# Sums of a graph attention layer in four PSUM banks instead of six, and seams between the stages of a transformer kernel

## The chip, the core and the metric

The kernel runs on one core of a Trainium2 chip. A core has TensorE for matrix products, VectorE, ScalarE and GpSimd for elementwise work, SyncE, which here issues all transfers, and 16 DMA engines. Products go to PSUM, eight banks of 2 KB for each of the 128 partitions; everything else lies in SBUF, which all engines read. The metric is the device time of one execution in microseconds. In the profile PE is TensorE's matmul, PEld its loading of weights, DVE is VectorE, ACT ScalarE, POOL GpSimd and SP SyncE. L1234 is line 1234 of the kernel.

## The reference, cut to what matters

There are 4096 nodes with 256 features each and one adjacency matrix of 4096 x 4096. Two graph attention (GAT) layers with 8 heads of 32 features come first, then one transformer layer in which only neighbours see each other.

```
def _gat_layer(x, adj_mat, W, a):                 # twice, with elu and a residual sum
    Wh = einsum('nd,hdo->hno', x, W)
    src = einsum('hno,ho->hn', Wh, a[:, :O]);  dst = einsum('hno,ho->hn', Wh, a[:, O:])
    e = leaky_relu(src[:, :, None] + dst[:, None, :], 0.2)
    e = where(adj_mat > 0, e, NEG_INF)
    alpha = softmax(e, axis=-1)
    out = einsum('hnm,hmo->hno', alpha, Wh)
...
    q, k, v = split(layer_norm(x, g1, be1) @ w_qkv)
    attn = softmax(where(adj != 0, (q @ k.T) * SCALE, -inf))
    x = x + (attn @ v) @ w_proj + b_proj
    return x + gelu(layer_norm(x, g2, be2) @ w1 + b1) @ w2 + b2
```

A leaky ReLU is one of two straight lines, so that exp(e) is a product of a factor of the row and a factor of the column on either side of a threshold. The kernel uses this: it never takes an exponential of a 4096 x 4096 matrix in the GAT layers. It makes a matrix of zeros and ones in fp8, `s`, which says where source plus destination is above zero and an edge exists, and sums values that have been multiplied by the column's factor beforehand.

## The kernel before

It has three stages: the two GAT layers, then the projection to queries, keys and values and the attention, then the output projection and the feed-forward part.

**GAT sums.** A block has 4 or 8 tiles of 128 rows. A pair of heads `p` and a block make eight groups `g` of four column tiles `m`. `vst` holds the values of a head, 132 columns in fp16: 66 of the high half (33 for either side of the threshold, of which one is the denominator) and 66 of the low half, which is what fp16 left out. In every tile and every `m`, four products are added up in PSUM. Each has a stationary operand of 128 x 128 fp8 (`s` of head 0, `s` of head 1 twice, the mask) that is loaded for it:

```
# L1188, g == 0
banks = -(-2 * tiles // 3)                        # 6 banks for 8 tiles
...
# L1219 to L1236, for n in tiles, for m in range(4)
todo = [
    (k_0, acc[k_0][:, o_0 : o_0 + 2 * VW], s_of_m[0], heads[:, 0, :]),     # 132 columns, high and low apart
    (k_1, acc[k_1][:, o_1 : o_1 + VW], s_of_m[1], heads[:, 1, :VW]),       # 66 columns, high
    (k_1, acc[k_1][:, o_1 : o_1 + VW], s_of_m[1], heads[:, 1, VW:]),       # 66 columns, low, same place
    (k_m, acc[k_m][...],  masks[l, nb][g][:, w, m, at], over),             # 132 columns, both heads
]
for i_, (k, to, left, right) in enumerate(todo):
    nc.tensor.matmul(to, left, right, start=k not in opened, stop=last)
...
# L1237 to L1250, in the last group, when a bank is complete: two copies for each bank
nc.scalar.copy(ev[0][...], acc[k][:, : (b - a) * 2 * VW])
nc.scalar.copy(ev[1][...], acc[k][:, start_at : start_at + (b - a) * VW])
...
# L1053, later: the halves that were kept apart are added
nc.vector.tensor_tensor(halves[:, :, :VW], halves[:, :, :VW], halves[:, :, VW:], op=ALU.add)
# L1061 to L1066: (over - sum1) * r + sum0, in five instructions
```

The `s` matrices come from `compare` (L1021 on ScalarE, L1023 on VectorE, and the bitwise L1026 with the mask), two groups ahead. In the first block of each layer, the values of the other columns are prepared between the sums: `features` (L916), `term_rows` (L926) and `values` (L942 to L972), one column tile at a time in one of two PSUM banks which the transposes of the mask (L849) use too. The weights of both layers are loaded and extended by DVE before anything else (L881 to L898).

**Projection and attention.** Four lines matter. SBUF is given out like a stack; the new pools lie where those of the GAT layers lay.

```
v_sb = vals.tile([P, NT, D], F32, name="u_v")
k_st = vals.tile([P, DC * HC, N], F16, name="u_k")
with ExitStack() as qkv:                          # weights, x, layer norm, halves, 8 PSUM banks
    nc.sync.dma_start(wq_sb, ...)                                         # L1398
    for nb in range(8):                           # 512 rows each
        ...                                       # layer norm and transposes two and one blocks ahead
        for i in (1, 0):                          # keys, then queries; L1419
            ...                                   # fp16 halves, written to DRAM (half_d)
            if i == 1: stack(k_st[:, :, cols], 1, (0, 0, 1, 1), cols)     # keys of this block read back
        ...                                       # values, L1440
blocks = tile_pool("u_blocks", bufs=2); masks = tile_pool("u_masks", bufs=5); work = ...
...
load_queries(0)                                   # L1387: read back from half_d
for k in range(4): load_chunk(0, k)               # L1467: masks
for i in range(len(units) + 5): ...               # attention: L1480, L1487, L1489, L1494, L1580
```

**Feed-forward.** Its weights are loaded when the attention's SBUF is free; `u_wp` is the third of them. The loop over eight blocks is L1628 to L1673.

Of the kernel before, what the change touches and what calls it, by code (L numbers as in the profile page):

```python
# [21 lines left out]
P = 128  # L22
# [726 lines left out]
def graph_attention(  # L749
# [19 lines left out]


# [16 lines left out]
    BW = 6 * VW  # L787
# [19 lines left out]
    vst = [keep.tile([P, G, H, 2 * VW], F16, name=f"vst{q}") for q in range(NG)]  # L807

# [68 lines left out]
    for l, (w, a) in enumerate(weights):  # L877
# [25 lines left out]
        L.tops = keep.tile([P, NT], F32, name=f"g_tops{l}")  # L903
# [33 lines left out]
    def values(l, q, t):  # L937

        L = layers[l]
        pv = turn_bank([P, 512], F32)  # L940
        for c in range(DC):
            nc.tensor.matmul(  # L942
                pv[:, : D + 2 * H],
                L.ft[q][:, c, t * P : (t + 1) * P],
                L.w_ext[:, c, :],
                start=(c == 0),
                stop=(c == DC - 1),
            )
        at = G * q + t
        nc.vector.tensor_scalar(  # L950
            L.negd[:, at, :], pv[:, D + H : D + 2 * H], -1.0, None, op0=ALU.mult
        )
        nc.scalar.activation(L.r[:, at, :], pv[:, D : D + H], AF.Exp, scale=LRELU - 1.0)
        nc.vector.tensor_reduce(
            L.tops[:, at : at + 1], pv[:, :D], AX.X, ALU.max, apply_absolute_value=True
        )

        prod = some.tile([P, H, 2, V1], F32, name="g_prod")
        big = some.tile([P, 2, H], F32, name="g_big")
        for i in range(2):  # L960
            nc.scalar.activation(big[:, i, :], L.negd[:, at, :], AF.Exp, scale=(-1.0, -LRELU)[i])
            nc.vector.tensor_scalar(prod[:, :, i, O], big[:, i, :], UP, None, op0=ALU.mult)
        nc.vector.tensor_tensor(
            prod[:, :, :, :O],
            pv[:, :D].rearrange("p (h o) -> p h o", o=O).unsqueeze(2).to_broadcast([P, H, 2, O]),
            prod[:, :, :, O : O + 1].to_broadcast([P, H, 2, O]),
            op=ALU.mult,
        )
        part = prod.rearrange("p h i v -> p h (i v)")
        halves = vst[q][:, t].rearrange("p h (k v) -> p h k v", k=2)  # L970
        nc.scalar.copy(halves[:, :, 0, :], part)
        nc.vector.tensor_tensor(halves[:, :, 1, :], part, halves[:, :, 0, :], op=ALU.subtract)  # L972

    def check_values(l):
        L = layers[l]
        for values_, bound in (
            (L.tops, VALUE_MAX),
            (L.negd.rearrange("p t h -> p (t h)"), DST_MAX),
            (L.r.rearrange("p t h -> p (t h)"), R_MAX),
        ):  # L980
            checks.below(some, values_, bound)

    def preparation(l, q):

        steps = [lambda: (term_rows(l, q), values(l, q, 0))]
        steps += [lambda t=t: values(l, q, t) for t in range(1, G)]
        if q + 1 < NG:
            steps.insert(0, lambda: features(l, q + 1))
        else:
            steps.append(lambda: check_values(l))  # L990
        return steps
# [39 lines left out]
    def pair_end(l, nb, p, ev):  # L1031
# [8 lines left out]
        broad, narrow = ev  # L1040
        broad = broad[:, : 2 * n].rearrange("p (t i) v -> p t i v", i=2)

        def block(name, last):
            return ep.tile([P, BT, 2, last], F32, name=name)[:, :n]

# [4 lines left out]
        def step_sum():  # L1050
            y = block("e_y", V1)
            halves = ev[0][:, : 2 * n]
            nc.vector.tensor_tensor(  # L1053
                halves[:, :, :VW], halves[:, :, :VW], halves[:, :, VW:], op=ALU.add
            )

            sums = ((broad[:, :, 1, :V1], broad[:, :, 1, V1:VW]),
                    (narrow[:, :n, :V1], narrow[:, :n, V1:]))
            for j in range(2):
                over = broad[:, :, 0, j * V1 : (j + 1) * V1]  # L1060
                nc.vector.tensor_tensor(y[:, :, j, :], over, sums[j][1], op=ALU.subtract)  # L1061
# [3 lines left out]
            for j in range(2):  # L1065
                nc.vector.tensor_tensor(y[:, :, j, :], y[:, :, j, :], sums[j][0], op=ALU.add)  # L1066
# [90 lines left out]
    for i, (l, nb, p, g) in enumerate(groups):  # L1157
        start = nb == 0 and p == 0
        if start and g == 0:

            features(l, 0)
# [15 lines left out]
        if start and g + 3 < NG:  # L1177
            slots = preparation(l, g + 3)
        beside(i)
# [11 lines left out]
        tiles = TILES[l][nb]  # L1191
        if g == 0:


            banks = -(-2 * tiles // 3)
            acc = [ps.tile([P, 512], F32, name=f"bank{k}") for k in range(banks)]
            place = []
            for n in range(tiles):
                spots = [divmod(2 * n + k, 3) for k in range(2)]
                spots = [(k, r * 2 * VW) for k, r in spots]  # L1200
                k = min(n, banks - 1)
                spots.append((k, BW if k < banks - 1 else 2 * VW * (2 * tiles - 3 * k) + (n - k) * VW))
                place.append(spots)
            until = [max(n for n in range(tiles) for k, _ in place[n] if k == b) for b in range(banks)]
            opened = set()
        if g == NG - 1:
            ev = (
                ep.tile([P, 2 * BT, 2 * VW], F32, name="ev_broad"),
                ep.tile([P, BT, VW], F32, name="ev_narrow"),
            )  # L1210
        for n in range(tiles):
            w, at = n // per, slice(n % per * P, (n % per + 1) * P)
            for m in range(G):
                s_of_m = [t8[:, j, w, m, at] for j in range(2)]
                heads = vst[g][:, m, 2 * p : 2 * p + 2]
                over = heads.rearrange("p j (k v) -> p k j v", k=2)[:, :, :, V1:]
                (k_m, o_m), (k_0, o_0), (k_1, o_1) = place[n]
                todo = [
                    (k_0, acc[k_0][:, o_0 : o_0 + 2 * VW], s_of_m[0], heads[:, 0, :]),  # L1219
                    (k_1, acc[k_1][:, o_1 : o_1 + VW], s_of_m[1], heads[:, 1, :VW]),  # L1220
                    (k_1, acc[k_1][:, o_1 : o_1 + VW], s_of_m[1], heads[:, 1, VW:]),
                    (
                        k_m,
                        acc[k_m][:, o_m : o_m + 2 * VW].rearrange(
                            "p (k j v) -> p k j v", k=2, j=2
                        ),
                        masks[l, nb][g][:, w, m, at],
                        over,
                    ),
                ]  # L1230
                for i_, (k, to, left, right) in enumerate(todo):
                    last = g == NG - 1 and m == G - 1 and until[k] == n
                    last = last and all(k != other[0] for other in todo[i_ + 1 :])
                    nc.tensor.matmul(to, left, right, start=k not in opened, stop=last)  # L1234
                    opened.add(k)
            if g == NG - 1:  # L1236
                for k in range(banks):  # L1237
# [523 lines left out]
```

## Time and profile before

The time is 3523.65 us, the median of 3 runs (3523.45 to 3526.0).

| stage | from to, us | what fills it |
|---|---|---|
| GAT, layer 1, with the mask turned beside it | 0 to 962 | PE, ACT and DVE in turn |
| GAT, layer 2 | 962 to 1784 | PE |
| projections | 1796 to 1893 | PE, in fp32 |
| attention | 1914 to 3228 | PE and DVE |
| feed-forward | 3239 to 3524 | PE |

In the profile's rows of groups, the number after "x" is a count, the first number after the bar is the time in which at least one of them ran, the second is the mean duration of one, in ns. Matmuls overlap their successors, so that the duration of one is longer than the distance between two; what a matmul costs is read from the distance. The column "idle before" gives how long the engine stood still just before them and what ended it. A table of windows gives for each stretch its busy time and number of instructions by engine, then the granted clock of TensorE as a share of full speed, then the mean busy share of the DMA engines and the GB/s.

### The profile page before, as it was taken

What the parts mean: (1) busy time and instruction counts of PE and PEld (TensorE: products, weight loads), DVE (VectorE), ACT (ScalarE), POOL (GpSimd) and SP (SyncE); (2) the same over time, 40 slices, a digit from 0 to 9 for tenths busy, and PEclk for the clock granted to TensorE, in tenths of its full rate; (3) what the DMA queues carried; (4) which work ended last, traced back from release to release, by engine and by line L of the source; (5) the groups of instructions that cost most, each with busy time, mean ns of one, the idle gap of its engine ahead of it and who ended that gap; (6) DMA issues with size and microseconds to landing.
All of it is one profiled execution on the core that took longest, in us unless ns stands there. A gap on an engine that the chain in (4) does not pass through costs nothing.

```text
span 3524.0 us, 99099 instructions
## 1 busy us (share of the span) xinstructions
PE 3357.4 (95%) x43715; PEld 2128.8 (60%) x43715; DVE 2903.2 (82%) x3580; ACT 2730.9 (77%) x3528; POOL 1239.1 (35%) x538
## 2 busy tenths in 40 slices
PE   6898999999989999999987999999999999997998
PEld 4698999999969999999963111111111121112666
DVE  5898999999889999999944999999999999996111
ACT  4799999998778888888854777777777777775332
POOL 0000000000000000000001999999999999996110
PEclk8999999999999999999998999999999999998999
DMA  4357554441221312111156010101010110002110
GB/s 140 123 191 242 167 167 157 157 123 39 68 62 33 86 39 80 45 58 37 26 135 171 10 40 13 37 19 31 25 25 25 25 37 13 28 9 68 44 47 25
DMA packets 199560, 252.76 MB, mean 72 GB/s; under 512 B 88080, under 2 KB 134672, under 8 KB 199120
## 3 DMA queue, kind: packets, MB, share of 16 engines
q1 hardware_dynamic: 199120, 246.34, 23.3%
q8 instruction: 344, 5.64, 0.7%
q14 instruction: 96, 0.79, 0.1%
HBM read 203.83 MB, written 42.47 MB: 70 GB/s over the span
## 4 chain that ended last, share of the span: by engine, by line
PE 73%; DVE 11%; ACT 9%; DMA 3%; issue 2%; POOL 2%; SPq 0%; DVEq 0%; ACTq 0%; POOLq 0%
PE bank L1234 34%; PE u_ps L1480 12%; PE u_av L1494 11%; PE u_dn L1494 6%; ACT t L1021 5%; DVE u_e L1489 4%; PE misc L1666 3%; PE misc L1419 2%; POOL u_both L1580 2%; DVE t L1023 1%; ACT u_ps L1487 1%; ACT stage L850 1%; DVE t L1026 1%; PE misc L1650 1%; PE turn L926 1%
## 5 line engine op out<-in xcount | busy, mean ns | idle before, releaser
L1234 PE MATMUL bank<-vst,t 128*128 128x66 f16 (+1 forms) x24576 | 1517.9, 203 | 22.0 <-DVE t L1026 15.5
L1234 PEld LDWEIGHTS <-t 128*128 128x128 fp8e4 x24576 | 1505.6, 97 | 33.2 <-DVE t L1026 18.0
L1234 PE MATMUL bank<-vst,mask 128*128 128x132 f16 x8192 | 1503.5, 222 | 0.0
L1021 ACT ACTIVATE t<-s_b,g_negd 128x1024 int8<-128x1024 f32 (+1 forms) x1296 | 1260.0, 1063 | 88.8 <-PE bank L1234 88.1
L1489 DVE SCALAR_TENSOR_TENSOR u_e<-u_mask,u_ps 128x1024 f32<-128x1024 uint8 x1024 | 1201.7, 1215 | 100.7 <-ACT u_ps L1487 95.8
L1580 POOL TENSOR_TENSOR u_both<-u_e 128x1024 f32<-128x1024 f32 x512 | 1199.8, 2367 | 238.5 <-DVE u_e L1489 238.3
L1487 ACT ACTIVATE u_ps<-u_ps 128x1024 f32<-128x1024 f32 x1024 | 1010.8, 1008 | 296.2 <-PE u_ps L1480 277.2
L1234 PEld LDWEIGHTS <-mask 128*128 128x128 fp8e4 x8192 | 803.6, 98 | 1.9 <-issue 0.9
L1026 DVE TENSOR_TENSOR t<-t,mask 128x2048 int32<-128x2048 int32 (+1 forms) x288 | 590.6, 2051 | 119.5 <-ACT t L1021 109.8
L1023 DVE TENSOR_SCALAR t<-s_b,g_negd 128x1024 fp8e4<-128x1024 f32 (+1 forms) x1008 | 638.5, 687 | 2.7 <-PE bank L1234 2.3
masks.py:197 POOL MEMSET u_ident<- 128x128 f32 x1 | 0.2, 204 | 1785.7 <-DMA u_wq<-in_L_gnn_w_qkv_dram 1785.7
L1480 PE MATMUL u_ps<-u_q,u_k 128*128 128x512 f16 x2048 | 580.5, 384 | 36.8 <-DMA u_q<-half_d 21.7
L1480 PEld LDWEIGHTS <-u_k 128*128 128x128 f16 x2048 | 139.2, 97 | 743.7 <-issue 685.4
L1494 PE MATMUL u_av<-u_e,u_v 128*32 128x512 f32 x4096 | 547.1, 605 | 0.0
L1494 PE MATMUL u_dn<-u_both,u_ones 128*32 128x512 f32 x2048 | 274.0, 605 | 1.3 <-POOL u_both L1580 1.3
L1494 PEld LDWEIGHTS u_av<-u_e,u_v 128*32 128x32 f32 x4096 | 80.9, 108 | 219.1 <-issue 211.3
L1657 ACT ACTIVATE u_hid<-misc,u_b 128x512 f32<-128x512 f32 x64 | 42.3, 683 | 142.9 <-PE misc L1650 142.8
L850 ACT ACTIVATE stage<-turn 128x1024 fp8e4<-128x1024 bf16 x112 | 114.2, 1037 | 1.1 <-PE turn L849 1.0
L1673 DVE TENSOR_TENSOR u_xres<-u_xres,misc 128x256 f32<-128x256 f32 x32 | 13.5, 421 | 122.7 <-PE misc L1666 122.7
L1666 PE MATMUL misc<-u_w,u_hid 128*128 128x256 f32 x512 | 111.8, 379 | 0.0
L1650 PE MATMUL misc<-ln_cols,u_w 128*128 128x512 f32 x256 | 111.2, 592 | 0.0
L1494 PEld LDWEIGHTS u_dn<-u_both,u_ones 128*32 128x32 f32 x2048 | 40.6, 108 | 110.9 <-issue 108.4
(104 smaller groups left out, 1749.8 us busy)
## 6 DMA issues: line engine op xcount, KB each, us to landing
g_rows<-in_adj_dram SPq DMA_DIRECT2D x128, 512.0 KB
mask<-mask SPq DMA_DIRECT2D x120, 256.0 KB
s_b<-s_d SPq DMA_DIRECT2D x56, 512.0 KB
u_mask<-mask SPq DMA_DIRECT2D x32, 512.0 KB
mask<-stage SPq DMA_DIRECT2D x28, 512.0 KB
half_d<-u_halves SPq DMA_DIRECT2D x32, 256.0 KB
u_k<-half_d SPq DMA_DIRECT2D x32, 256.0 KB
u_q<-half_d SPq DMA_DIRECT2D x32, 256.0 KB
```

What stands on the lines that cost most here:

```text
L850: nc.scalar.activation(staged[0].rearrange("p i g n -> p (i g) n")[:, :, t * P : (t + 1) * P], pt, AF.Identity, saturate=False,)
L1021: nc.scalar.activation(to.bitcast(I8), s, AF.Sign, bias=negd, scale=-1.0)
L1023: nc.vector.tensor_scalar(to, s, negd, None, op0=ALU.is_ge, saturate=False)
L1026: nc.vector.tensor_tensor(both, both, mask.unsqueeze(1).to_broadcast(list(both.shape)), op=ALU.bitwise_and)
L1234: nc.tensor.matmul(to, left, right, start=k not in opened, stop=last)
L1480: nc.tensor.matmul(ps[:, j, :], k_st[:, h, mt * P : (mt + 1) * P], q_st[:, h, :], start=True, stop=True,)
L1487: nc.scalar.activation(ps, ps, AF.Exp, scale=SCALE)
L1489: nc.vector.scalar_tensor_tensor(e, mask, 0.0, ps, op0=ALU.not_equal, op1=ALU.mult)
L1494: nc.tensor.matmul(to[j * O : (j + 1) * O, :], lefts[j], es[j // 2][:, j % 2, :], start=start, stop=stop,)
L1580: nc.gpsimd.tensor_tensor(both, es_of[i - 1][u], es_of[i][u], op=ALU.add)
L1650: nc.tensor.matmul(ph, w1_sb[:, k, f * P : (f + 1) * P], hn[:, k, :], start=(k == 0), stop=(k == DC - 1),)
L1666: nc.tensor.matmul(po[:, :D], hid[:, f, at : at + P], w2_sb[:, f, :], start=(f == 0), stop=(f == FC - 1),)
```

## The change

It replaces one arrangement of the sums with another and moves loads at the borders of the stages.

- **Sums.** Four banks of two tiles each. All products have 66 columns: high and low of either head are added in PSUM, and so are high and low of the mask's product. That is six products in place of four, and as many columns (396). One copy takes a bank out; the addition of the halves on DVE falls away.
- **Values.** Two column tiles at once, in a pair of banks of their own (the two that the sums gave up).
- **Weights.** Those of layer 2 are prepared in the second block of layer 1.
- **Seams.** Keys are read back one block later; queries and masks of the first attention block are loaded within the projection loop; their pools come before those of the projection, whose pools then lie in the part of SBUF that held the adjacency rows. `halves` gets a third buffer. The feed-forward's pools are reordered and its `u_wp` is loaded first.

```
-    BW = 6 * VW
+    SW = 3 * VW
+    def two_banks():
+        return ps.tile([P, 2, 512], F32, name="two")
...
-    for l, (w, a) in enumerate(weights):
+    def weights_of(l):
...
-    def values(l, q, t):
+    def values(l, q, half):
-        pv = turn_bank([P, 512], F32)
+        pv = two_banks()
...
+            if l == 0:
+                weights_of(0)
...
+        if l + 1 < NL and nb == 1 and p == 0 and g == 0:
+            weights_of(l + 1)
...
-            banks = -(-2 * tiles // 3)
...
+            acc = [ps.tile([P, 512], F32, name=f"bank{k}") for k in range(TILES[l][nb] // 2)]
...
+            sums = acc[n // 2][:, n % 2 * SW : (n % 2 + 1) * SW]
             for m in range(G):
...
+                for j in range(2):
+                    for k in range(2):
+                        nc.tensor.matmul(
+                            sums[:, j * VW : (j + 1) * VW],
+                            t8[:, j, w, m, at],
+                            vst[g][:, m, 2 * p + j, k * VW : (k + 1) * VW], ...
+                for k in range(2):
+                    nc.tensor.matmul(
+                        sums[:, 2 * VW :].rearrange("p (j v) -> p j v", j=2),
+                        masks[l, nb][g][:, w, m, at],
+                        vst[g][:, m, 2 * p : 2 * p + 2, k * VW + V1 : (k + 1) * VW], ...
+            if g == NG - 1 and n % 2 == 1:
+                nc.scalar.copy(ev[:, n - 1 : n + 1]..., acc[n // 2][:, : 2 * SW])
...
+        k_st = vals.tile([P, DC * HC, N], F16, name="u_k")
         v_sb = vals.tile([P, NT, D], F32, name="u_v")
-        k_st = vals.tile([P, DC * HC, N], F16, name="u_k")
+        blocks = scope.enter_context(tc.tile_pool(name="u_blocks", bufs=2))
+        masks = scope.enter_context(tc.tile_pool(name="u_masks", bufs=5))
...
-                    if i == 1:
-                        stack(k_st[:, :, cols], 1, (0, 0, 1, 1), cols)
...
+                for b in (nb - 1,) if nb + 1 < NNB else (nb - 1, nb):
+                    if b >= 0:
+                        at = slice(b * NB, (b + 1) * NB)
+                        stack(k_st[:, :, at], 1, (0, 0, 1, 1), at)
+                    if b == 0:
+                        load_queries(0)
+                if 2 <= nb < 2 + NT // MC:
+                    load_chunk(0, nb - 2)
...
-        load_queries(0)
-        for k in range(NT // MC):
-            load_chunk(0, k)
...
+        wp_sb = big.tile([P, DC, D], F32, name="u_wp")
+        nc.sync.dma_start(wp_sb, w_proj.rearrange("(c p) e -> p c e", p=P))
```

## Prediction

> **What bounds the kernel now.** I read the page's busy shares first, then a table of windows to see which engine is full where, then the timeline to price one product, and last the waits of PE, which show the seams.
>
> ```profile
> PE 3357.4 (95%) x43715; PEld 2128.8 (60%) x43715; DVE 2903.2 (82%) x3580; ACT 2730.9 (77%) x3528; POOL 1239.1 (35%) x538
> ...
> PE bank L1234 34%; PE u_ps L1480 12%; PE u_av L1494 11%; PE u_dn L1494 6%; ACT t L1021 5%; DVE u_e L1489 4%; PE misc L1666 3%; PE misc L1419 2%; POOL u_both L1580 2%; DVE t L1023 1%; ACT u_ps L1487 1%; ACT stage L850 1%; DVE t L1026 1%; PE misc L1650 1%; PE turn L926 1%
> ```
>
> PE is busy for 95% of the span, and the chain of work that ended last runs over the GAT sums (L1234) for a third of it. A busy PE in this view need not be at its peak, so the windows come next.
>
> ```profile
> 0.00:100.00 100.00, 64.41 (x481) 42.93 (x482) 61.06 (x171) 51.39 (x130) 1.08 (x8) 0.90 0.44 134
> 100.00:200.00 100.00, 84.62 (x1287) 71.91 (x1285) 86.25 (x203) 82.91 (x166) 0.00 (x0) 0.93 0.48 158
> 200.00:400.00 200.00, 182.56 (x3753) 178.78 (x3751) 184.11 (x341) 198.11 (x306) 0.00 (x0) 0.97 0.62 201
> 400.00:900.00 500.00, 498.15 (x10788) 495.90 (x10786) 461.38 (x552) 468.89 (x552) 0.00 (x0) 1.00 0.41 128
> 900.00:1100.00 200.00, 187.22 (x2986) 159.35 (x2984) 173.34 (x331) 152.68 (x288) 0.00 (x0) 0.98 0.20 61
> 1100.00:1783.00 683.00, 682.98 (x14959) 681.38 (x14957) 613.67 (x704) 596.64 (x709) 0.00 (x0) 1.00 0.18 51
> ```
>
> After each stretch and its length stand PE, PEld, DVE, ACT and POOL. From 400 to 900 and from 1100 to 1783 us PE has no gap while ACT and DVE have 6 to 13%. From 200 to 400 us ACT is the full one (198 of 200), and PE has 17 us to spare. Before 200 us and around 970 us nothing is full: those are the preparations.
>
> The timeline gives the price of the four products of one tile and one `m`:
>
> ```profile
> 1001.00 0.28 PE L1234 MATMUL bank<-vst,t 128*128 128x132 f16 x3
> 1001.12 0.22 PE L1234 MATMUL bank<-vst,mask 128*128 128x132 f16 x1
> 1001.18 0.28 PE L1234 MATMUL bank<-vst,t 128*128 128x132 f16 x3
> 1001.30 0.22 PE L1234 MATMUL bank<-vst,mask 128*128 128x132 f16 x1
> 1001.36 0.28 PE L1234 MATMUL bank<-vst,t 128*128 128x132 f16 x3
> ```
>
> Every 0.18 us a new set begins; the mask's product starts 0.12 us into it. Read record by record between 1200 and 1700 us, the distances from start to start are 56.7 ns after the 132-column product, 33.4 ns and 32.5 ns after the two of 66, and 60.0 ns after the mask's 132: together 182.6 ns.
>
> The seams are in the list of what PE waited for:
>
> ```profile
> PE u_ps L1480 <- DMA u_q<-half_d: 21.7, 1, 21.7
> PE misc L1365 <- ACT ln_square L1341: 12.7, 1, 12.7
> PE misc L1628 <- DMA u_att<-att_d: 11.9, 1, 11.9
> PE bank L1234 <- ACT ev_narrow L1246: 6.3, 7, 1.3
> ```
>
> 21.7 us before the attention, 12.7 us before the projections, 11.9 us before the feed-forward, each once.
>
> **What the skill says.** The page "TensorE: Matmul & The Clock Gate", section "Wait — 56ns, not 53.3ns?", gives N/2.4 GHz plus about 2.5 ns between matmuls at full clock: 30.0 ns for 66 columns, 57.5 ns for 132. The trace has 32.5 to 33.4 and 56.7 to 60.0; I take the trace's. The same page, "Step-by-step: what each phase is for", says that the next weights are loaded while a matmul runs, through a port of their own. The trace agrees: each load's record begins about 2 ns after the start of the matmul before its own, and even a 66-column product hides it. "Weight-path perf modes — Fast Weight Load (FWL) and DoubleRow" mentions about 40 ns for a small fp8 matmul with its load; the trace's 33 ns is less. "Part 1: The HAM clock gate (the "warmup" mystery)" says that some 3.4 us of idleness halve the clock; here the granted clock reads 0.50 from 1900 to 1920 us, within and after the 21.7 us gap.
>
> **The change part by part.**
>
> *Sums.* Six products of 66 columns replace 132, 66, 66 and 132. The columns stay at 396, so what is paid is the fixed part of two more products with two more loads. In the new order products come in pairs with equal stationary operand and equal destination, then change: exactly the pattern of the two existing 66-column ones. So a set costs 3 x (33.4 + 32.5) = 197.8 ns, 15.2 ns more than 182.6. The instructions of L1234 in the windows, divided by four, are 2581 sets from 400 to 900 us and 3742 from 1100 to the end. There PE has no slack: 6323 x 15.2 ns = +96 us.
>
> *200 to 400 us, ACT-bound.* 856 sets cost PE 13 us more; it had 17 us spare. ACT gets lighter: for a four-tile block a pair of heads paid two copies of 396 columns at 506 ns, one of 264 at 404 ns and three narrow ones of 243, 243 and 302 ns, 2.2 us; now two of about 0.51 us. That is 1.2 us in a pair that lasts about 30 us, 4%. PE takes the place of ACT as the bound, nearly full from both sides: I put +4 us.
>
> *900 to 1100 us.* 690 sets cost 10 us; about half lies in PE's 13 us of gaps, and DVE's preparation gets shorter (below): +5 us.
>
> *0 to 200 us.* First sums start at 51 us, at the end of a serial chain. DVE no longer works through layer 2's weights first, eight instructions of 0.42 us (3.4 us), and the first x no longer waits for the buffers that they held; it was issued at 10.2 us. I put -4 us. Values in pairs save fixed costs on DVE: per pair of column tiles one `g_negd` (159 ns) and about 150 ns of a `g_tops` (416 ns) and two of four small multiplications (166 ns each), 0.64 us of 4.4; but the pair of banks is single, so PE must wait until DVE has read both halves. Net -2 us. In sum -6 us.
>
> *Ends of pairs.* The last copies come in four steps with nothing left to add. Of the 6.3 us waited for the narrow copy I take back 4. The 40 us that DVE spent on L1053 is off the path.
>
> *GAT to projections.* The weights come long before. But x must still wait: `u_x` lies in a pool that reaches 224 bytes into the last `t8` buffer, and in the built program its load still waits for the last sums. What goes away is the 768 KB of weights ahead of it and the second x that was issued 6 us after the first; also DVE reaches the layer norm about 1.5 us sooner, since the pair's end is three instructions of 0.7 us rather than six of 3.6 us together. The chain of mean, four squares (2.5 us), table load (1.3 us) and scaling stays. -4 us.
>
> *Projections to attention.* Queries and masks are in SBUF by then. PE can start the first scores about 1 us after its last value product. The first masked weights must wait until the last fp16 halves are in DRAM, since their buffers overlie `u_halves`: the last of those transfers took 6.2 us, behind a cast and a subtraction of 1.3 us that end about 2 us before the last value product. So DVE begins about 5 us after PE's last projection, not 23.8 us (1892.6 to 1916.4): -19 us.
>
> *Attention to feed-forward.* The wait of 11.9 us is for `u_att`, issued behind the last denominators and large weights in both programs; an earlier `u_wp` does not move it. 0 us.
>
> Sum: 96 + 4 + 5 - 6 - 4 - 4 - 19 = +72 us: 3524 + 72 = 3596 us, +2.0%.
>
> **Rivals.** *(a) The load becomes the bound.* With six loads in 198 ns there is no long product left behind which a slow load could hide. If a set of 66 columns cost the 40 ns of the skill's figure, it would take 240 ns and the GAT stage some 360 us more, near 3880 us. Against it: between two adjacent 66-column products there is one load already, issued only after the first began, and the distance is 33 ns. I give it 5%. *(b) The lighter ACT and DVE win.* 142 us of copies on ACT become about 65, 40 us of DVE's additions vanish. If these engines set the pace also in the PE-full stretches, through waits that show as PE's, the sums' cost would be half hidden: some 3545 us. Against it: from 1100 to 1783 us PE has no gap at all, and ACT waits for PE there (88 us before L1021). 12%. *(c) The seam is hidden anyway or collides.* Three megabytes of queries and masks move into the projection loop, where the DMA engines are already 70% busy; if x or the halves came late, PE's 89 us there would stretch, and if eight key loads at the end slow the last halves, 5 us become 10 us. Then +5 to +10 us, about 3603 us. 25%. *(d) PE stalls in the preparations* at the single pair of banks, in order, with sums behind it: 16 preparations of 1 to 3 us, +15 to +40 us in part of which PE is idle anyway. 20%.
>
> **Range and chances.** The large term is counts that are sure times a distance known to about 2 ns per set, 13 us. The preparations and the seams are uncertain by 10 us each. Eight in ten: 3562 to 3622 us. The border of 2% lies at 3594 us, on my estimate. Slower by over 2%: 0.52; within 2%: 0.46; faster by over 2%: 0.02.
>
> **What would show it.** In the new profile, 49152 products of 66 columns, at 198 ns per six between 1100 and the end of the GAT stage, whose length there grows by 57 us; 195 or 201 ns move the result by 18 us each way. The copies of L1240 and L1246 are one row of 128 at about 0.5 us. ACT is below 95% from 200 to 400 us and PE above 97%. PE's list of waits no longer has 21.7 us for `u_q`, but about 5 us for `u_e` or a transfer; the wait of the first layer norm is 8 to 12 us; the one for `u_att` remains about 12 us. The prediction is wrong if six products take clearly more or less than 198 ns, or if PE waits over 15 us in all for the pair of banks.

## The result, and the profile after

The changed kernel takes 3552.61 us (median of 4 runs, 3551.84 to 3564.22), against 3523.55 us for the kernel before beside it: a ratio of 1.0091, 95% interval 1.0068 to 1.0113. It is 29 us slower, where the prediction said 72 us. The time lies below the range of 3562 to 3622 us, and errors of opposite sign cancel in part in that sum.

The page of the changed kernel, its busy shares and its chain of work that ended last:

```profile
PE 3395.4 (96%) x60099; PEld 2182.1 (61%) x60099; DVE 2858.0 (81%) x3344; ACT 2684.1 (76%) x3176; POOL 1239.0 (35%) x538
...
PE bank L1209 26%; PE bank L1217 13%; PE u_ps L1467 12%; PE u_av L1481 12%; PE u_dn L1481 6%; DVE u_e L1476 4%; PE misc L1650 3%; ACT t L1027 3%; PE misc L1415 2%; PE two L947 1%; ACT u_ps L1474 1%; POOL u_both L1564 1%; PE turn L850 1%; ACT stage L851 1%; PE misc L1434 1%
```

PE has 16384 products more and is busy for 38 us more; DVE and ACT have 45 and 47 us less to do. The sums (now L1209 for `s` and L1217 for the mask) take 39% of the chain instead of 34%.

The table of windows over the GAT stage (length, then busy time of PE, PEld, DVE, ACT and POOL, the granted clock, the share of the DMA engines, GB/s):

```profile
0.00:100.00 100.00, 75.65 (x743) 51.52 (x744) 67.92 (x149) 58.72 (x123) 1.08 (x8) 0.93 0.53 158
100.00:200.00 100.00, 88.41 (x2343) 84.50 (x2343) 94.73 (x197) 90.85 (x153) 0.00 (x0) 0.97 0.59 184
200.00:400.00 200.00, 182.46 (x5358) 180.24 (x5355) 175.94 (x301) 187.93 (x262) 0.00 (x0) 0.98 0.62 200
400.00:900.00 500.00, 494.70 (x15369) 493.84 (x15366) 433.80 (x503) 439.25 (x455) 0.00 (x0) 1.00 0.38 120
900.00:1100.00 200.00, 184.49 (x4212) 161.13 (x4209) 162.59 (x253) 141.61 (x213) 0.00 (x0) 0.98 0.21 65
1100.00:1815.00 715.00, 711.43 (x22604) 710.62 (x22601) 599.72 (x666) 583.13 (x595) 0.00 (x0) 1.00 0.17 50
```

Three things differ from the table of before. The first 100 us hold 743 products where they held 481 (76 sets of sums and 64, as a set has six products now). ACT is no longer full from 200 to 400 us (188 of 200, it was 198). And from 1100 us on PE has 3.6 us of gaps where it had none.

The timeline of PE shows the new sets, one every 0.19 us, with four products of `s` and then two of the mask:

```profile
1200.01 0.29 PE L1209 MATMUL bank<-vst,t 128*128 128x66 f16 x4
1200.14 0.22 PE L1217 MATMUL bank<-vst,mask 128*128 128x66 f16 x2
1200.20 0.29 PE L1209 MATMUL bank<-vst,t 128*128 128x66 f16 x4
1200.33 0.22 PE L1217 MATMUL bank<-vst,mask 128*128 128x66 f16 x2
1200.39 0.29 PE L1209 MATMUL bank<-vst,t 128*128 128x66 f16 x4
```

Read record by record in the second GAT layer, the distances from start to start are 29.3, 34.4, 32.5 and 32.3 ns for `s` and 30.0 and 30.0 ns for the mask: 188.6 ns, not the 197.8 of the prediction. Before, the same reading gives 182.1 ns.

What PE waited for:

```profile
PE misc L1343 <- DVE ln_rows L1327: 36.1, 10, 11.0
...
PE misc L1612 <- issue: 12.2, 1, 12.2
PE bank L1209 <- issue: 11.1, 11, 2.2
PE two L947 <- ACT vst L978: 10.3, 10, 1.9
PE bank L1217 <- issue: 7.6, 7, 2.3
PE bank L1209 <- ACT ev L1225: 7.4, 5, 3.1
...
PE two L947 <- DVE g_prod L969: 7.0, 11, 1.7
```

The 21.7 us for `u_q` are gone. In their place stand 36.1 us for the layer norm (`ln_rows`): 11.0 us at the start of the projections, and 15.7 us inside the loop (26.7 us in all from 1826 to 1944 us), where the kernel before had 1.3; the rest belongs to the feed-forward. The waits of the sums for "issue" (nothing that the profile shows) are new: 18.7 us in all. PE waits 17.3 us for the pair of banks (`two`, the two lines of the list).

Where the 26 us between the two profiled executions (3524.0 and 3550.0 us) arise:

| stage | before, us | after, us | difference |
|---|---|---|---|
| start to the end of the first set of sums | 51.5 | 52.5 | +1.0 |
| from there to the hundredth set | 89.6 | 61.5 | -28.1 |
| hundredth set to the end of the GAT stage | 1642.5 | 1701.8 | +59.3 |
| to the first transpose of the projections | 12.7 | 11.0 | -1.7 |
| projection loop | 96.2 | 115.3 | +19.1 |
| to the first scores | 21.7 | 0.5 | -21.2 |
| attention, output projection and feed-forward | 1609.8 | 1607.4 | -2.4 |

So three questions remain: why the sums cost less than a count of pairs says, why the preparation of layer 1 gained 28 us, and what lengthened the projection loop.

### The profile page after: what moved, and what is told of

Read it like the earlier page. It is cut to its first block, busy times and chain, and to the rows that moved or that the text cites. A ratio compares the mean times of both kernels' runs of the same rounds, so it can differ in the third digit from the quotient of the medians.

```text
span 3550.0 us, 131328 instructions
## 1 busy us (share of the span) xinstructions
PE 3395.4 (96%) x60099; PEld 2182.1 (61%) x60099; DVE 2858.0 (81%) x3344; ACT 2684.1 (76%) x3176; POOL 1239.0 (35%) x538
## 3 DMA queue, kind: packets, MB, share of 16 engines
q1 hardware_dynamic: 199120, 246.34, 23.1%
q8 instruction: 472, 7.73, 0.9%
## 4 chain that ended last, share of the span: by engine, by line
PE 79%; DVE 8%; ACT 7%; issue 3%; DMA 2%; POOL 1%; SPq 0%; DVEq 0%; ACTq 0%; POOLq 0%
PE bank L1209 26%; PE bank L1217 13%; PE u_ps L1467 12%; PE u_av L1481 12%; PE u_dn L1481 6%; DVE u_e L1476 4%; PE misc L1650 3%; ACT t L1027 3%; PE misc L1415 2%; PE two L947 1%; ACT u_ps L1474 1%; POOL u_both L1564 1%; PE turn L850 1%; ACT stage L851 1%; PE misc L1434 1%
## 5 line engine op out<-in xcount | busy, mean ns | idle before, releaser
L1209 PE MATMUL bank<-vst,t 128*128 128x66 f16 x32768 | 1567.6, 194 | 25.2 <-issue 11.1
L1209 PEld LDWEIGHTS <-t 128*128 128x128 fp8e4 x32768 | 1554.3, 98 | 33.3 <-issue 23.3
L1217 PE MATMUL bank<-vst,mask 128*128 128x66 f16 x16384 | 1554.9, 193 | 7.8 <-issue 7.6
L1217 PEld LDWEIGHTS <-mask 128*128 128x128 fp8e4 x16384 | 1049.4, 97 | 11.6 <-issue 11.1
```

Of the source, the lines that this page charges most:

```text
L1209: nc.tensor.matmul(sums[:, j * VW : (j + 1) * VW], t8[:, j, w, m, at], vst[g][:, m, 2 * p + j, k * VW : (k + 1) * VW], start=first and j = ...
L1217: nc.tensor.matmul(sums[:, 2 * VW :].rearrange("p (j v) -> p j v", j=2), masks[l, nb][g][:, w, m, at], vst[g][:, m, 2 * p : 2 * p + 2, k * ...
```

## The experiments

All times are medians beside the kernel before, which stayed between 3522.1 and 3524.6 us; the ratio is to it. Versions with six products in a set scatter more than the others: twenty executions of one of them (`six`, below) took 3518 to 3538 us, the kernel before beside it 3522 to 3527 us. In five profiles whose GAT stage is the same (the changed kernel, `seams_old`, `ln3`, `keys_now`, `x8`) that stage ends between 1810 and 1828 us. So a few microseconds between two such profiles mean nothing.

**1. The old seams behind the new sums** (`seams_old`). Edit:

```
-def unshifted_transformer(...)   # of the changed kernel
+def unshifted_transformer(...)   # of the kernel before, unchanged
```

> The new sums, values and weights, with the old seams from the layer norm on. Theory (the ledger of the two traces: the new seams cost 19.2 us in the projection loop and 1.7 to 2 us less at the start of it and in the feed-forward, and save 21.3 us before the attention): about 3557 us, 4 us above the changed kernel, with a projection loop of 96 us and 21 us of waiting before the attention. Rival (the two are one thing: the loop is longer because the GAT stage leaves SBUF or transfers in another state): the loop stays at 115 us and the wait comes back as well, about 3573 us.

Measured: 3553.2 us (1.0095, 1.0078 to 1.0111), the time of the changed kernel. The loop is back at 95.3 us and the wait before the attention at 21.4 us. The two belong together: they come and go with the new seams, and as they stand the new seams are worth next to nothing. Without the scatter of the GAT stage, from its end on, the two profiles differ by 5.6 us (1739.8 us here, 1734.2 in the changed kernel). The reverse, **the old GAT stage with the new seams** (`gat_old`, with three buffers for the layer norm), says the same.

> The GAT stage of before (four products in a set, values one at a time, weights first), with the new seams and three buffers in the pools of the layer norm. If the new seams save the 21 us before the attention and lose nothing in the loop with three buffers: 3523 - 21 - 2 = about 3500 us. If the loop stays at 115 us: about 3520 us.

Measured: 3523.83 us (1.0001, 0.9992 to 1.0009), loop 116.0 us, gap 0.5 us. The second of the two cases holds; from the end of the GAT stage on it is 1737.9 us, against 1740.4 in the kernel before.

**2. What lengthens the loop: buffers of the layer norm** (`ln3`) **or the keys in SyncE's queue** (`keys_now`). Edits:

```
-ln = ... tile_pool(name="u_ln", bufs=2);  lnc = ... tile_pool(name="u_lnc", bufs=2)
+ln = ... tile_pool(name="u_ln", bufs=3);  lnc = ... tile_pool(name="u_lnc", bufs=3)
```

```
+if i == 1: stack(k_st[:, :, cols], 1, (0, 0, 1, 1), cols)     # at once
-for b in (nb - 1,) if ...: stack(k_st[:, :, at], ...)          # a block later
```

> The changed kernel with three buffers instead of two in the two pools of the layer norm of the projection loop. Theory (the loop takes 115 us and not 96 because with two buffers x and the layer norm can only be one block ahead): the loop falls to about 96 us, the time by 19 us to about 3533 us. Rival (the loads of x come late because they stand in SyncE's queue behind the halves, the keys and the queries): no change, 3550 to 3555 us, loop 115 us.

> The changed kernel with the keys of a block read back at once, as before; queries and masks stay in the loop. Theory (buffers of the layer norm): no change of the loop, 115 us. Rival (the later keys in SyncE's queue hold back x): the loop falls towards 96 us, the time to 3535 to 3545 us.

Measured: 3555.08 us (1.0088, 1.0071 to 1.0105) with a loop of 116.9 us, and 3563.43 us (1.0104, 1.0084 to 1.0124) with a loop of 121.5 us. Both ideas fall. The timeline of DVE in the changed kernel, within one block of the loop, shows what is going on (start, duration, operation; in brackets the idle time before it and what ended it):

```profile
1877.65 0.69 DVE L1423 TENSOR_TENSOR u_halves<-misc,u_halves 128x512 f16<-128x512 f32 x1 [1.02 <-ACT u_halves L1422]
1878.26 1.21 DVE L1314 TENSOR_REDUCE ln_mean<-u_x 128x4 f32<-128x1024 f32 x1
1879.50 0.17 DVE L1315 TENSOR_SCALAR ln_mean<-ln_mean 128x4 f32<-128x4 f32 x1
1883.62 0.18 DVE L1324 RECIPROCAL ln_dev<-ln_dev 128x4 f32<-128x4 f32 x1 [3.95 <-ACT ln_dev L1323]
1883.90 1.38 DVE L1327 TENSOR_SCALAR ln_rows<-u_x,ln_mean,ln_dev 128x256 f32<-128x256 f32 x4
1889.68 0.69 DVE L1423 TENSOR_TENSOR u_halves<-misc,u_halves 128x512 f16<-128x512 f32 x1 [4.39 <-ACT u_halves L1422]
```

The mean starts right behind the last half of the block before, without waiting for `u_x`. Its x had been issued at 1863.55 us, 15 us earlier. The transfer is not late; the layer norm stands late in the order of instructions, which is fixed before the kernel runs, and PE transposes its rows at once. One block of the loop is then a chain: projections, last half, mean, four squares on ACT, rows, transposes, projections. It takes 17.2 us where it took 11.2. In the kernel before, the layer norm of blocks 4 to 7 stands one to two blocks ahead in the same order. In the changed kernel the load of x of block 4 stands in SyncE's order behind the halves of block 1 and the queries, and each later one behind the halves and keys of another block, so that its layer norm is put behind them too.

**3. Eight buffers for x** (`x8`). Edit:

```
-some = ... tile_pool(name="u_qkv", bufs=2)      # holds only u_x
+some = ... tile_pool(name="u_qkv", bufs=8)
```

> The changed kernel with eight buffers for x in the projection loop instead of two; nothing else. In its built order SyncE then issues x before the halves and queries that it stood behind, and DVE and ACT have the layer norm one to two blocks ahead. Theory (the loop is long because the fixed order of instructions has the layer norm of blocks 4 to 7 just in front of its use, so that PE waits for it): loop back to about 96 us, time 3552 - 19 = about 3534 us. Rival (the traffic of queries and masks, or the waits of the halves, stretch the loop): loop stays at 112 to 116 us, time 3550 to 3555 us.

Measured: 3542.9 us (1.0056, 1.0039 to 1.0073); the loop takes 93.1 us. SyncE's timeline has every x but one ahead of the first halves, and PE's waits for the rows in the loop are down from 15.7 to 0.6 us:

```profile
1837.64 0.50 SPq L740 DMA_DIRECT2D u_x<-rows  x1
...
1838.91 0.38 SPq L740 DMA_DIRECT2D u_x<-rows  x1
...
1848.46 1.81 SPq L1427 DMA_DIRECT2D half_d<-u_halves  x2
1850.32 0.47 SPq L740 DMA_DIRECT2D u_x<-rows  x1
```

The cause of the longer loop is shown: 22 us come back for one number. The time fell by only 10 us. (The profile is of an execution of 3553.86 us, whose GAT stage took 12 us longer than in the changed kernel's profile; from the end of that stage on it, too, is 10 us shorter.) The waits at the start of the attention show what takes the rest away:

```profile
DVE u_e L1476 <- DMA half_d<-u_halves: 8.7, 1, 8.7
PE u_ps L1467 <- DVE u_e L1476: 7.3, 2, 6.9
PE u_ps L1467 <- DMA half_d<-u_halves: 5.0, 1, 5.0
```

With the loop short, the masked weights wait for the last halves on their way to DRAM, whose SBUF they overlie. PE's first scores come 4.5 us later and the attention takes 7 us longer than in the changed kernel. The prediction had foreseen this wait, with DVE at work about 5 us after PE's last projection; here it is 13.3 us, and 3.5 us in the changed kernel, whose long loop had hidden it.

**4. What the preparation gained: banks or pairs.** The values one column tile at a time, in the banks shared with the turns of the mask (`values_old`), or one at a time in two banks of their own (`values_own`):

```
-pv = two_banks()                                                    # two tiles, one pair of banks
+pv = turn_bank([P, 512], F32)                                       # values_old
+pv = ps.tile([P, 512], F32, name="own", tag="own", bufs=2)          # values_own
```

> The changed kernel with the values of one column tile at a time in the two banks shared with the turns of the mask, as before; the pair of own banks is unused. Theory (the 27 us that the start of layer 1 gained come from the values in pairs with banks of their own): 20 to 27 us slower than the changed kernel, 3573 to 3580 us, all of it in the first 120 us. Rival (they come from the weights of layer 2 that no longer stand ahead of everything, and from lighter copies): within 5 us of the changed kernel.

> The changed kernel with the values of one column tile at a time, but in two banks of their own. If the gain at the start is that of the banks (PE and DVE no longer wait for each other's turns of the mask): within 5 us of the changed kernel. If it is that of the pairing (fewer instructions on DVE and ACT): 15 to 27 us slower, as with the shared banks.

Measured: 3576.8 us (1.0143, 1.0126 to 1.016) and 3538.75 us (1.0048, 1.0031 to 1.0065). Shared banks cost 24 us against the changed kernel, so the gain was in the values. But values one at a time in own banks are 14 us *faster* than in pairs: the pairing costs, the banks gain. Little of that arises at the start: the first set is complete at 44.5 us instead of 52.5, yet the hundredth begins at 112.5 and 113.8 us. Another 5.4 us arise between the sums of the two layers (31.5 us instead of 36.9), where layer 2's first values are prepared; the other 6 us lie spread over the sums, within their scatter. Then **the same on the kernel before, alone** (`gat_own`): layer 1's first block has four tiles and fills three of six banks, and two of the idle ones take the values.

```
-pv = turn_bank([P, 512], F32)
+if l == 0: pv = ps.tile([P, 512], F32, name=f"bank{3 + t % 2}")
+else:      pv = turn_bank([P, 512], F32)
```

> The kernel before, with one edit: in layer 1 the values of a column tile are computed in two PSUM banks that the first block does not use (it has four tiles and fills three of six banks) instead of the two shared with the turns of the mask. If the gain of 21 to 27 us between the first and the hundredth set is that of banks of their own: 3523 - 22 = about 3501 us. If it needs the lazy weights or the new sums: 3515 to 3524 us.

Measured: 3491.54 us (0.9916, 0.9899 to 0.9932), 31 us faster by this edit alone, 9 more than forecast; 28.5 us of it are there at the hundredth set. The waits between 50 and 150 us show why. First the kernel before, then this one (the waits of most time):

```profile
DVE g_negd L950 <- PE turn L942: 26.6, 5, 8.7
ACT g_ft L919 <- PE turn L916: 16.7, 7, 6.3
ACT g_rows L934 <- PE turn L926: 11.6, 6, 3.3
```

```profile
ACT g_ft L919 <- PE turn L916: 5.1, 3, 3.0
PEld L1237 <- DVE t L1029: 4.0, 2, 3.5
...
DVE g_negd L953 <- PE bank L945: 1.5, 3, 0.6
```

DVE had stood for 26.6 us because the value products had to wait for a bank that a turn of the mask held. That wait is down to 1.5 us, and most of ACT's is gone.

**5. The price of a set.** Values stored so that all six products move two runs of 33 columns (`runs33`); the order high of head 0, high of head 1, low, low, then the mask (`alternate`); and the mask's high half between them (`mid`):

```
-vst[g][:, m, 2 * p + j, k * VW : (k + 1) * VW]                                        # runs33
+vst[g][:, m, 2 * p + j].rearrange("p (i k v) -> p i k v", i=2, k=2)[:, :, k, :]
```

```
-for j in range(2): for k in range(2): s(j, k)      ; for k in range(2): mask(k)
+for k in range(2): for j in range(2): s(j, k)      ; for k in range(2): mask(k)       # alternate
+for k in range(2): { for j in range(2): s(j, k); mask(k) }                            # mid
```

> The changed kernel with the values stored so that the four products of s move their 66 columns as two runs of 33, as the two products of the mask do, into two runs of 33. In the changed kernel the mask's products stand 30.0 ns apart and those of s 29.3, 34.4, 32.5 and 32.4 ns. Theory (the shape of the moving operand makes the difference): all six at 30.0 ns, a set at 180 ns and not 188.6 ns, 50 to 70 us faster, about 3490 us. Rival (the place in the order, or the fp8 comparison result as stationary operand, makes it): a set stays at 188 to 189 ns and the time at 3550 to 3555 us.

> The changed kernel with the four products of s in the order high of head 0, high of head 1, low of head 0, low of head 1, so that no product adds to the place of the one before it and none loads the same stationary operand as the one before it. Theory (the 8.6 ns by which a set of six exceeds six times 30.0 ns come from adding twice in a row to one place): a set at 180 to 184 ns, 35 to 65 us faster. Rival (they come with each set, from the step from the mask back to s or from the supply of instructions): 188.6 ns, 3550 to 3555 us.

> The changed kernel with the six products of a set in the order high of head 0, high of head 1, high of the mask, and then the low halves likewise: no stationary operand and no destination twice in a row. Theory A (each product after one with the same stationary operand or place costs extra): a set at 180 ns. Theory B (TensorE is near the rate at which instructions reach it: the faster a set, the more it waits with no releaser shown, as in the order tried before, where the set fell by 4.7 ns and those waits grew from 19 to 37 us): whatever the set's price, its mean with those waits stays above 185 ns, and the waits grow if the price falls. Time between 3520 and 3550 us under both; only the split differs.

| version | distances, ns | set, ns | waits for "issue" in the sums, us | time, us | ratio, 95% interval |
|---|---|---|---|---|---|
| changed kernel | 29.3, 34.4, 32.5, 32.3, 30.0, 30.0 | 188.6 | 18.7 | 3552.61 | 1.0068 to 1.0113 |
| `runs33` | 30.0, 33.5, 35.0, 30.0, 30.0, 30.0 | 188.6 | 23.1 | 3547.71 | 1.0049 to 1.0082 |
| `alternate` | 29.3, 35.3, 29.3, 29.8, 30.1, 30.1 | 183.9 | 37.5 | 3534.39 | 1.0021 to 1.0037 |
| `mid` | 29.2, 31.7, 30.0, 29.2, 32.7, 30.2 | 183.0 | 33.0 | 3524.83 | 0.9999 to 1.0018 |

The shape is not it: the distances move, the set stays. The order is part of it: in `mid`, with neither a stationary operand nor a place twice in a row, a set is 5.6 ns shorter. These orders change the two together, so they do not tell which of them counts. `alternate` gained 18 us, half of the least that its theory gave. The set does not fall to 180 ns, so theory A of `mid` explains only part. With the waits the mean of `mid` over the last 3072 sets, all in layer 2, is 184.4 ns (566.4 us), a little below the 185 ns that theory B set. B's waits did grow with the faster orders. Neither theory is settled by this alone; what ends the waits is read in experiment 7.

**6. The parts together, and the sums alone.** The sums of before with banks for layer 1's values, the weights of layer 2 later, the new seams and eight buffers for x (`best2`); then with the last block's halves in a lent buffer (`lent`); then that version with the changed kernel's six products (`six`) and with the order of `mid` (`six_mid`).

```
+if nb + 1 == NNB: lent = blocks.tile([P, DC * HC, NB], F16, name="u_q")                       # lent
+    halves = lent[:, 2 * DC * i : 2 * DC * (i + 1)].rearrange("p (k c) n -> p k c n", k=2)
```

> The sums of before (four products in a set), values in banks of their own in layer 1, weights of layer 2 in the second block, the new seams, and eight buffers for x. If the parts add up: 3523 - 22 (banks) - 7 (weights, first set) - 23 (seams without the longer loop) = about 3471 us. If the loop stays at 116 us: about 3491 us.

> The version with four products, own banks, new seams and eight buffers for x, with one more edit: the halves of the last block of the projections lie in the second buffer of the queries, so that the first masked weights of the attention, whose buffers overlie the halves, wait for block 6's transfers only. Theory (the 5.1 us before the first scores and the 7 us by which the attention is longer are the wait for the last block's halves on their way to DRAM): 8 to 12 us less than 3479.6, 3468 to 3472 us. Rival (the DMA engines are full with the keys and queries anyway): within 3 us of 3479.6.

> The same seams, banks and weights as the version with lent halves, but with the six products of the changed kernel. It prices the sums alone. Theory (8192 sets at 188.6 instead of 182.1 ns, +53 us, and 15 to 25 us of waits with no releaser, less what the preparations hide): 50 to 70 us slower than the version with four products. Rival (lighter copies and no additions on DVE give part of it back): 30 to 45 us slower.

> As the six-product version beside it, with the order high of head 0, high of head 1, high of the mask, then the low halves. If orders add up as measured before: 28 us faster than that version. Against the version with four products: still 20 to 35 us slower, because the instructions, not the products, set its pace.

| version | time, us | ratio, 95% interval |
|---|---|---|
| `best2` | 3479.61 | 0.9882, 0.9866 to 0.9899 |
| `lent` | 3469.56 | 0.9848, 0.9831 to 0.9864 |
| `six` | 3525.76 | 1.0006, 0.9999 to 1.0014 |
| `six_mid` | 3493.91 | 0.9914, 0.9894 to 0.9934 |

One of the four executions of `six_mid` took 4698.64 us at a granted clock of 0.65, in a slow state, and is left out.

`best2` misses its sum by 9 us, although the banks alone had given 31 us and not the 22 put in: weights and seams gave 12 us instead of 30. The wait for the halves is 10.1 us of that, which `lent` takes off, as its theory had it. The loop of `lent` is 93.3 us, the gap 2.6 us, the attention 1311.8 us, and DVE begins 5.0 us after PE's last projection. Later weights do not add up with the banks: the first set is complete 6 us sooner than in `gat_own`, but the GAT stage ends at 1752.7 instead of 1751.2 us. `lent` beats both kernels of this study.

`six` against `lent` prices the new sums, lighter copies included: 3525.76 - 3469.56 = 56.2 us. One thing besides the sums differs: the four banks of `six` leave two for the values of layer 2 as well, which in `lent` still share with the turns, and between the sums of the two layers `six` is 4.8 us faster (31.5 against 36.3 us).

The price is less than the set (53 us) and the 17.7 us of waits for "issue" together. From the 327th to the 1183rd set, where ACT was the full engine, `six` loses 5.4 us, though the sets alone make 5.6 us and 7.5 us of the waits lie there. The rival, in which the lighter DVE and ACT bring it down to 30 to 45 us, is out in this pair; `values_own` against `gat_own`, where seams and weights differ too, gives 47.2 us.

`six_mid` is 31.9 us faster than `six`, but still 24.4 us behind four products; of these some 7 us are the set (183.0 against 182.1 ns), and the 30.1 us of waits for "issue" are more than enough for the rest.

**7. Five products** (`five`): in `lent`, only the product of head 0 split in two.

```
-(k_0, acc[k_0][:, o_0 : o_0 + 2 * VW], s_of_m[0], heads[:, 0, :])
+(k_0, acc[k_0][:, o_0 : o_0 + VW], s_of_m[0], heads[:, 0, :VW])
+(k_0, acc[k_0][:, o_0 + VW : o_0 + 2 * VW], s_of_m[0], heads[:, 0, VW:])
```

> The version with four products and lent halves, with the product of head 0 (132 columns) split into high and low, 66 columns each, into the two places where they went before: five products and five loads in a set, the same columns. Theory (the waits with no releaser come when TensorE takes its instructions faster than they arrive; 8 in 182 ns give none, 12 in 188 ns give 15 to 26 us, 12 in 183 ns 30 to 37 us): 10 in about 185 ns give less than 8 us of such waits, and the time is 15 to 35 us above 3469.6. Rival (they come with loading equal stationary operands twice or with 66-column products as such): 10 us or more of them.

Measured: 3522.6 us (0.9998, 0.9989 to 1.0006), 53 us above `lent`, where the theory said 15 to 35: five products cost nearly what six cost. The distances are 29.2, 34.1, 32.6, 32.5 and 59.9 ns, together 188.3. So 6.2 of the set's extra 6.5 ns are there once head 0's product is split (56.7 ns in one, 63.3 in two), and splitting the mask's as well adds 0.1 ns (59.9 in one, 60.0 in two). Here the halves of head 0 go to two places, in `six` to one (63.9 ns): adding twice in a row to one place is not what makes the pair dear. And the waits that the theory put below 8 us:

```profile
PE bank L1243 <- issue: 12.1, 15, 1.7
```

With 10 instructions in 188 ns they are 12.1 us, hardly less than the 17.7 us of `six` with 12. The number of instructions per time does not explain them by itself. Traffic does not either: in `six` 11.1 of the 17.7 us fall between 200 and 450 us, where the DMA engines are at 0.60, and 0.5 us between 1200 and 1740, where they are at 0.18; but in `x8` 9.1 of 26.4 us fall in that last stretch.

What ends these waits can be read from the packets of the queue that brings TensorE's instructions. It carries 7.73 MB after, 6.68 MB in `five` and 5.64 MB before, in 472, 408 and 344 packets of 16 KB; TensorE's records in these traces, divided by the packets, are about 255 in each of the three. In the changed kernel all 18 waits end 1.2 to 1.6 us after such a packet has landed, and in the 13 versions with five or six products 345 of 347 end 1.1 to 1.7 us after one. A moment picked at random between the sums lies so in 11 to 14 of 100 cases. These packets are late ones: in the changed kernel one starts 4.0 us after the one before it in the median, those that end a wait 5.9 us; in `five` it is 4.9 and 7.7 us. So TensorE stood still until its next instructions had come. Why a packet starts late no run shows.

## Why the prediction was wrong

The direction was right; the size came out too large by 43 us. Point by point:

- **Price of a set: the step that failed most.** The step was "exactly the pattern of the two existing 66-column ones. So a set costs 3 x (33.4 + 32.5)". Head 1's pair is near that (65.9 ns before, 64.8 after), but head 0's pair takes 63.7 and the mask's 60.0 ns: 188.6 in place of 197.8 ns, +6.5 a set and not +15.2. The price of one product was carried over to others by resemblance. The Trainium skill's "TensorE: Matmul & The Clock Gate", section "Wait — 56ns, not 53.3ns?", which the prediction named and set aside for the trace's pair, gives by its formula an estimate of 30.0 ns for 66 columns; the mask's products here stand at 30.0, those of `s` between 29.3 and 34.4. Each of the two figures fits some of the products and neither fits all.
- **The sums as a term.** The prediction's +96, +4 and +5, less 4 for the ends of pairs, are +101; by `six` against `lent` they measure +56.2. The sets alone make 8192 x 6.5 ns = 53 us. The waits for "issue" were not in the sum at all. The ends of pairs gave nothing back: PE waits 7.4 us for `ev`, where it waited 6.3 for `ev_narrow`. In the ACT-bound stretch the sets from 327 to 1183 took 200.2 us before and 204.8 after, which looks like the +4; but in `seams_old`, with the same GAT stage, they took 200.4, so this does not confirm it. ACT fell to 94% as said, and PE did not become nearly full there (182 of 200). The 88 us for which ACT waits for PE, named against rival (b), are those of the whole execution; 58.2 us lie between 1100 and 1783 us.
- **Preparation of layer 1, -6 predicted.** The trace has -27 us at the hundredth set. The step "Values in pairs save fixed costs on DVE ... net -2" counted instructions of DVE, and not that DVE stood for 26.6 us behind the turns of the mask in the shared banks. The own banks are the gain (-31 us on the kernel before), and pairing gives 14 us of it back. PE's waits for the pair are 17.3 us, past the 15 us that the prediction had named as a sign of being wrong; rival (d) was right that the single pair stalls PE, and the gain outweighed it.
- **Start, -4.** Right in kind: later weights bring the end of the first set from 51.3 us (`gat_own`) to 45.0 us (`best2`). With pairs it comes at 52.5 us in the changed kernel's profile and at 48 to 50 us in the seven others with pairs. But it does not carry to the end, as `best2` shows.
- **GAT to projections, -4.** -1.7 us: right in kind.
- **The projection loop: absent from the sum.** Rival (c) saw it stretch by late x or halves and gave 5 to 10 us. It stretched by 19 us, and not through traffic: eight buffers for x take it away with all the traffic left in; the order of instructions, read without times, already has the layer norm behind the halves. The prediction looked at waits and buffers there and not at that order.
- **Projections to attention, -19.** -21.2 us measured. The mechanism was right, the wait for the halves included; it appears once the loop is short, at 13.3 us from PE's last projection to DVE's start in `x8`, where the prediction had 5. But the gain was given back in the loop, so that the new seams give 0.0 us in time (`gat_old`).
- **Attention to feed-forward, 0.** 11.9 and 12.2 us: right.

So two errors went one way, 45 us too many for the sums and 21 too few gained in the preparation, and one the other, 19 us lost in a loop that was not in the sum. That the total missed by no more than 43 us is luck of these signs. The single effects do not add up exactly either: 56 for the sums, 31 less for own banks, 14 more for pairs and 0 for the seams make +39, and +29 was measured; the scatter of the versions with six products is as large as that.

## What to carry to other kernels

Before a transfer is moved to an earlier place, look at where it and everything behind it end up in each engine's order, and give the early stages enough buffers that their work is not pushed back; one number of buffers was worth 22 us in the loop and 10 us of the time. Two users that take turns at a pair of PSUM banks can cost more than either user's instructions: idle banks of a small block are worth 31 us here. And a product's price is to be read for that product, in its place; a split that looks free by one formula and dear by another may be both, as the mask's and head 0's were.

## What was unexpected in the hardware

- Products of 66 columns have no single price: 29.3 to 35.3 ns in one set (`alternate`), depending on place and order. An order that repeats neither stationary operand nor place took a set from 188.6 to 183.0 ns. Why, no run shows.
- TensorE can run ahead of the supply of its own instructions. Waits for "issue" of 12 to 37 us in the sums are in every version with five or six products and in none with four, and 345 of 347 end just after a packet of TensorE's instruction queue has landed.
- A 132-column product split in two costs 6.6 ns for `s` and 0.1 ns for the mask, although in both the two halves share the stationary operand.
